# One partial sum kept in its PSUM bank, the third chunk turned first, and one count raised, in a two-layer graph network on one core

## The chip, the cores and the metric

One core of a Trainium2 chip runs the whole program; the other cores are idle. The metric is the device time of one execution in microseconds, as the median of the executions. The kernel before takes 3694.73 us (four runs beside the changed kernel, 3692.88 to 3697.72). All four, and the four of the changed kernel, are in the fast state (in the other state, called slow, a run shows a lower granted clock; one later run of the kernel before is of that kind: 5324.52 us at a clock of 0.653, against 0.991 to 0.993 in the fast runs beside it). The engines are called PE (TensorE, the matrix products), DVE (VectorE), ACT (ScalarE), POOL or GpSimd, and SP, which issues most DMA transfers.

## The reference

32 graphs of 512 nodes with 512 features, one sparse adjacency matrix for all. Two layers, each with a normalisation, ReLU, and a residual:

```python
# layer 0: attention with 8 heads of 64, masked by adj
h = maximum(layernorm(x), 0)
q, k, v = h@Wq+bq, h@Wk+bk, h@Wv+bv            # (512 x 512) @ (512 x 512) each
scores = q·k / 8 + (1 - adj) * -1e9
x = x + (softmax(scores) · v) @ Wo + bo
# layer 1: attention of the GAT kind
h = maximum(layernorm(x), 0)
hw = h @ W
e = leaky_relu(hw@a1 [:,None] + hw@a2 [None,:], 0.2) * adj
x = x + elu(softmax(e) @ hw + beta * hw)
```

All arithmetic is f32. The biases are zero in the given inputs, which one experiment below makes use of.

## The kernel before

The kernel is a software pipeline over the 32 items. In the steady state one step works on four items at once, in an order given by a string:

```python
order = {...}.get(b, "0.VDU1.rgY2.RMNH3.KQ")
# digits 0-3: a "unit": values of the last head pair, scores of this one (4 blocks of 2 heads)
# V, K, Q, M (out-projection), Y (final product): seven half-size products (Strassen's kind) each
# N: transposes of the next item   D: diagonal   g: gather   r, R: load of the residual, halves 0 and 1
# U, H: GpSimd's sums of blocks for the seven products
```

So the stretch that matters reads: final product Y, unit 2 (values, scores), the residual's second half R, out-projection M, transposes N, unit 3. PE's accumulators are PSUM banks with the tags `x`, `y`, `qz` (used by the products of seven and by scores), `s`, `po`, `pd`.

The transposes (`turn`) make four chunks: 0 and 1 in one bank pair, 2 in `po`, 3 in `qz`. ACT evicts each with a ReLU:

```python
def second():
    for c, tag in ((2, "po"), (3, "qz")):
        p = psum.tile(..., tag=tag)
        turned(p, c)                                        # 4 transposes
        nc.scalar.activation(h[1][:, c - 2, :], p, AF.Relu)
def first():
    p = psum.tile([P, 2, N], F32, tag="s")
    for c in range(2):
        turned(p[:, c, :], c)
    nc.scalar.activation(h[0], p, AF.Relu)
first(); second()
```

The final product (`final`) ends each block with an ELU. `two` first adds a second product q, into an SBUF tile of the tag `y`, which has three slots:

```python
def elu(i, k, s):
    y = wtile([P, N], tag="y", bufs=3)
    for t in range(2):
        nc.scalar.activation(y[half t], s[half t], AF.Exp, scale=...)     # L811
    nc.vector.tensor_scalar(y, y, 1.0, -1.0, min, add)                     # L814
    for t in range(2):
        nc.vector.scalar_tensor_tensor(y[half t], s[half t], ..., y[half t], mult, max)   # L816
    ...   # GpSimd adds the residual (L824), SP stores it
def two(i, k, p, q):
    s = wtile([P, N], tag="y", bufs=3)
    nc.vector.tensor_tensor(s, p, q, op=add)                               # L836
    dve(0.75)
    elu(i, k, s)
```

`dve()` runs nothing. The program is recorded once, in Python, and the recorder keeps a model clock of PE and DVE. Work that may be done at leisure is put on a list (`later(key, wait, by, cost, fn)`), and `pe()` and `dve()` advance the clocks and take from that list what fits. So a number in `dve()` sets only the order of the instructions on DVE. On that list stand, among others, the normalisations of the next item (L359), the sums of the exponentials (`es`, L579), the reciprocal of the softmax denominators in two halves (L628), and the dot products of layer 1.

The other lines that are used below: the out-projection adds its products to the residual on DVE (L675); GpSimd adds a constant row to the residual as it lands (L654), adds one of the seven products to it (L691), and makes a block sum that the last out-projection product reads (L399).

## Time and profile before

| | before |
|---|---|
| device time, median of 4 | 3694.73 us |
| span of the profiled execution | 3693.4 us |
| PE busy | 3568.2 us (97%) |
| PE not busy | 125.2 us |
| mean granted clock of TensorE | 0.991 |
| unit 2, scores, of an ordinary item | 4.84 us |
| unit 3, scores, of the same kind and size | 3.63 us |
| out-projection, of an ordinary item | 12.19 us |

The last three rows are read from the timeline of PE: the start of PE's first instruction of a phase to the start of its first instruction of the next phase, as the median of the 28 ordinary items. This start-to-start figure holds all of a delay, whether or not the profile lists a wait for it. It is the ruler of this document. The main lines of the page and of the waits are in the prediction below. What it does not show is the stretch behind unit 2, so here it is, first PE (start, duration, operation), in an ordinary item of the kernel before:

```profile
1631.23 1.08 PE L620 MATMUL pd<-es,ones 128*64 128x512 f32 x4
...
1642.50 1.90 PE L53 MATMUL qz_w<-wo,uT 128*64 128x256 f32 x16
```

The first line, the denominators' matmul, is called P0 from here on. The second is the last product of the out-projection, at P0 + 11.27. It needs the bank `qz`, which DVE has to empty first, and the block sum `uT` of GpSimd. Now DVE and GpSimd in the same stretch:

```profile
1633.50 2.30 DVE L579 TENSOR_TENSOR es<-e,e 128x1024 f32<-128x1024 f32 x1
1635.90 3.44 DVE L579 TENSOR_TENSOR es<-es,e 128x1024 f32<-128x1024 f32 x2
1639.26 1.75 DVE L628 RECIPROCAL rd<-pd 128x256 f32<-128x256 f32 x1
1640.93 0.62 DVE L675 SCALAR_TENSOR_TENSOR x<-x_w,x 128x512 f32<-128x512 f32 x1
1641.47 0.67 DVE L675 SCALAR_TENSOR_TENSOR x<-qz_w,x 128x512 f32<-128x512 f32 x1
```

```profile
1632.18 2.54 POOL L654 TENSOR_TENSOR x<-x,c_row 128x512 f32<-128x512 f32 x2 [1.78 <-DMA x<-in_x_dram]
1636.55 3.91 POOL L691 TENSOR_TENSOR x<-x,q_w 128x512 f32<-128x512 f32 x2 [1.84 <-ACT q_w L456]
1640.43 1.27 POOL L399 TENSOR_TENSOR uT<-uT,oT 128x512 f32<-128x512 f32 x1
```

DVE has no idle time here. It empties `qz` at 1641.47 + 0.67 = 1642.14, that is P0 + 10.91, and PE wants it at + 11.27. The slack is 0.36 us here, 0.30 to 0.55 in the other ordinary items at full clock (0.65 in the two at half the clock). Of it some 0.2 can be used: where DVE is the one that PE waits for, as below, PE starts 0.15 us after it. GpSimd's block sum ends at 1640.43 + 1.27 = 1641.70, P0 + 10.47, a slack of 0.80. No list of waits shows either.

One more thing about that list. The records of PE's products overlap: in an unbroken row each is 1.90 us long, but they start 1.73 apart. The list counts a wait from the end of the record before it, so it leaves out the first 0.17 us of every delay, and it drops what then comes to 0.15 or less.

### The profile page before, as it was taken

To read this page: it belongs to the slowest core of one execution; us is meant where nothing else is said; L and a number is where in the kernel's file an instruction comes from. 1 tells how busy PE (TensorE), PEld (TensorE's weight loads), DVE (VectorE), ACT (ScalarE), POOL (GpSimd) and SP (SyncE) were. 2 spreads that over 40 slices of the span, in tenths; PEclk is the share of its full clock that TensorE was granted. 3 is DMA by queue.
4 is the path that set the end of the run, shared out by engine and by line. 5 is a ranking of instruction groups with operands and counts; after the bars stand their busy time and mean duration, and the time that the engine had idled before them with its cause. 6 is when DMAs were issued, how large, how long until landed. Compare 5 with 4: busy or idle time off the path is not lost. (4 is left out here: it accounts for less than half of the span.)

```text
span 3693.4 us, 62550 instructions
## 1 busy us (share of the span) xinstructions
PE 3568.2 (97%) x25845; PEld 1977.7 (54%) x25846; DVE 2948.4 (80%) x4335; ACT 1460.8 (40%) x2310; POOL 1392.8 (38%) x1090
## 2 busy tenths in 40 slices
PE   9999999999999999999999999999999999999986
PEld 5455555555555555545555555555555555555543
DVE  7988788888887787788788887878888878878774
ACT  3333334344433444343444334444434444343432
POOL 5433244333344332443333443334433334433241
PEclk9999999999999999999999999999999999999998
DMA  3000111001111001110011110011100111100100
GB/s 129 18 26 17 38 38 35 27 17 36 38 38 35 23 19 38 38 35 27 15 38 38 38 35 22 20 38 38 35 27 18 35 38 38 35 27 15 33 26 27
DMA packets 88034, 120.81 MB, mean 33 GB/s; under 512 B 11904, under 2 KB 49792, under 8 KB 87744
## 3 DMA queue, kind: packets, MB, share of 16 engines
q1 hardware_dynamic: 86160, 114.91, 10.0%
q8 instruction: 205, 3.36, 0.4%
q10 hardware_dynamic: 1376, 1.57, 0.1%
q14 instruction: 85, 0.70, 0.1%
q0 software_dynamic: 208, 0.27, 0.0%
HBM read 83.11 MB, written 33.62 MB: 32 GB/s over the span
## 5 line engine op out<-in xcount | busy, mean ns | idle before, releaser
L634 POOL TENSOR_TENSOR oT<-oT,rd 128x512 f32<-128x512 f32 x128 | 173.1, 1352 | 1489.3 <-ACT rd L633 1489.3
L582 ACT ACTIVATE e<-e 128x1024 f32<-128x1024 f32 x512 | 534.4, 1055 | 190.9 <-DVE e L567 164.8
L555 PE MATMUL ps<-qT,kT 64*128 64x512 f32 x2048 | 497.4, 613 | 41.2 <-DVE y L816 29.6
L567 DVE SCALAR_TENSOR_TENSOR e<-maskT,ps 128x1024 f32<-128x1024 uint8 x384 | 454.4, 1211 | 84.2 <-PE ps L555 84.0
L605 PE MATMUL po<-e,v 128*64 128x512 f32 x2048 | 463.7, 594 | 22.6 <-ACT hT L415 22.6
L53 PE MATMUL pg<-at,hn 128*64 128x512 f32 x2048 | 448.8, 597 | 4.2 <-DVE dmax L788 2.1
L628 DVE RECIPROCAL rd<-pd 128x256 f32<-128x256 f32 x256 | 434.0, 1725 | 1.2 <-POOL oT L634 1.2
L579 DVE TENSOR_TENSOR es<-es,e 128x1024 f32<-128x1024 f32 x254 | 396.6, 1562 | 18.5 <-ACT e L582 1.6
L555 PEld LDWEIGHTS ps<-qT,kT 64*128 64x128 f32 x2048 | 180.4, 186 | 354.3 <-issue 219.9
L53 PEld LDWEIGHTS pg<-at,hn 128*64 128x64 f32 x2048 | 148.7, 138 | 297.8 <-issue 289.2
L605 PEld LDWEIGHTS po<-e,v 128*64 128x64 f32 x2048 | 149.1, 138 | 253.5 <-issue 214.2
L824 POOL TENSOR_TENSOR y<-y,x 128x512 f32<-128x512 f32 x124 | 157.6, 1271 | 250.9 <-DVE y L816 210.4
L654 POOL TENSOR_TENSOR x<-x,c_row 128x512 f32<-128x512 f32 x124 | 221.7, 1809 | 52.1 <-DMA x<-in_x_dram 52.1
L814 DVE TENSOR_SCALAR y<-y 128x512 f32<-128x512 f32 x128 | 61.1, 478 | 207.7 <-ACT y L811 207.7
L633 ACT ACTIVATE rd<-rd 128x512 f32<-128x512 f32 x128 | 80.7, 630 | 348.7 <-DVE rd L628 348.7
L579 DVE TENSOR_TENSOR es<-e,e 128x1024 f32<-128x1024 f32 x127 | 189.9, 1495 | 1.5 <-PE pd L620 1.5
L756 ACT ACTIVATE at<-at 128x512 f32<-128x512 f32 x128 | 80.4, 628 | 257.7 <-DVE at L752 255.1
L53 PE MATMUL qz_y<-w,vT 128*64 128x256 f32 x1520 | 180.3, 379 | 2.0 <-DVE yq L836 2.0
L729 DVE CUSTOM_DVE_ANT_0 scr<-hn,wa_r 128x512 f32<-128x512 f32 x256 | 165.6, 710 | 0.0
L562 DVE SCALAR_TENSOR_TENSOR e<-maskT,ps 128x512 f32<-128x512 uint8 x256 | 163.4, 680 | 0.0
L802 ACT COPY gT<-pg 128x512 f32<-128x512 f32 x128 | 74.3, 581 | 213.6 <-PE pg L53 213.6
L334 POOL TENSOR_TENSOR rs<-rs,mhalf 128x2 f32<-128x2 f32 (+1 forms) x97 | 78.1, 805 | 206.0 <-DVE rs L333 202.4
(221 smaller groups left out, 6470.9 us busy)
## 6 DMA issues: line engine op xcount, KB each, us to landing
x<-in_x_dram SPq DMA_DIRECT2D x128, 256.0 KB, 3.3
out_dram<-y SPq DMA_DIRECT2D x128, 256.0 KB, 2.3
x<-in_x_dram SPq DMA_DIRECT2D x63, 512.0 KB, 3.8
s<-row_s SPq DMA_DIRECT2D x32, 256.0 KB, 4.0
adj<-in_adj_dram SPq DMA_DIRECT2D x4, 256.0 KB, 7.1
wk<-in_L_gnn_Wk_dram ACTq DMA_DIRECT2D x3, 256.0 KB, 9.0
wq<-in_L_gnn_Wq_dram SPq DMA_DIRECT2D x3, 256.0 KB, 7.0
wv<-in_L_gnn_Wv_dram SPq DMA_DIRECT2D x3, 256.0 KB, 5.9
```

What stands on the lines that cost most here:

```text
L53: nc.tensor.matmul(out[s : s + HD], lhsT[:, s : s + HD], rhs, start=start, stop=stop, skip_group_check=onto)
L555: nc.tensor.matmul(ps[s], st["kT"][j][rows, ts(k, P)], st["qT"][j][rows, :], start=True, stop=True)
L562: nc.vector.scalar_tensor_tensor(e[:, s, :], maskT[:, k, :], NEG, ps[s], op0=ALU.mult, op1=ALU.add)
L567: nc.vector.scalar_tensor_tensor(e, maskT[:, k, :].unsqueeze(1).to_broadcast([P, 2, N]), NEG, p, op0=ALU.mult, op1=ALU.add)
L579: (nc.gpsimd if early else nc.vector).tensor_tensor(es, one, e, op=ALU.add)
L582: nc.scalar.activation(e, e, AF.Exp)
L605: nc.tensor.matmul(po[s * HD : (s + 1) * HD, :], v[k // 2][:, k % 2, (2 * j + s) * HD : (2 * j + s + 1) * HD], e[k][:, s, :], start=k == 0 ...
L628: nc.vector.reciprocal(rd[:, ts(k, H)], pd[:, ts(k, H)])
L634: nc.gpsimd.tensor_tensor(o, o, rd, op=ALU.mult)
L654: eng.tensor_tensor(r[:, t, :], r[:, t, :], c_row, op=ALU.add)
L729: nc.vector.tensor_tensor_reduce(scr, st["hn"][t], r, 1.0, 0.0, op0=ALU.mult, op1=ALU.add, accum_out=st["s12"][:, g, t : t + 1],)
L824: (nc.vector if b == B - 2 else nc.gpsimd).tensor_tensor(yu, yu, x_[:, :, ts(i, H)], op=ALU.add)
```

## The change

The intent: take away the two largest waits of PE. The transposes are reordered so that the bank `po` is emptied early. The sum for block (0,1) is written back into its PSUM bank, so that one tile fewer competes for the three `y` slots. And the diagonal is counted as 3.0 us instead of 2.0, which moves DVE's leisure work to later places.

```diff
-        def second():
-            for c, tag in ((2, "po"), (3, "qz")):
-                p = psum.tile([P, 1 if c == 2 else 2, N], F32, name=f"pn{c}_{b}", tag=tag)[:, 0, :]
-                turned(p, c)
-                nc.scalar.activation(h[1][:, c - 2, :], p, AF.Relu)
+        def second(c, tag):
+            p = psum.tile([P, 1 if c == 2 else 2, N], F32, name=f"pn{c}_{b}", tag=tag)[:, 0, :]
+            turned(p, c)
+            nc.scalar.activation(h[1][:, c - 2, :], p, AF.Relu)
 ... (first() unchanged)
+        if b:
+            second(2, "po")
         first()
-        second()
+        if not b:
+            second(2, "po")
+        second(3, "qz")
 ... (in diagonal)
-        dve(2.0)
+        dve(3.0)
 ... (in final)
         def two(i, k, p, q):
-            s = wtile([P, N], f"yq_{b}_{i}_{k}", "y", 3)
+
+            s = p if i == 0 else wtile([P, N], f"yq_{b}_{i}_{k}", "y", 3)
```

In the changed kernel nearly all later line numbers are higher by 3: L555 becomes L558, L567 L570, L579 L582, L628 L631, L654 L657, L675 L678, L691 L694, L811 L814, L816 L819. L836 becomes L840 and L415 L414.

## The prediction

A dip of the clock, below, is a stretch in which PE's granted clock (PEclk) is 0.50 instead of 1.00; the trace before has two in mid-run, each of 3.4 us, after waits of PE of 1.96 and 2.04 us.

> **What bounds the kernel now.** First the page of the profiled execution, for the busy shares:
>
> ```profile
> PE 3568.2 (97%) x25845; PEld 1977.7 (54%) x25846; DVE 2948.4 (80%) x4335; ACT 1460.8 (40%) x2310; POOL 1392.8 (38%) x1090
> ```
>
> PE is busy 97% of 3693.4 us, and the change adds and removes no matmul (PE's order differs only in which transposed chunk goes first). What can be won is PE's idle time, 3693.4 - 3568.2 = 125.2 us, 3.4%. So the second view is who PE waited for (total us, times, longest):
>
> ```profile
> PE ps L555 <- DVE y L816: 29.6, 29, 2.0
> PE po L605 <- ACT hT L415: 22.6, 31, 0.8
> PE pe L53 <- DVE as L763: 19.1, 2, 11.7
> PE ps L555 <- DVE e L567: 11.6, 31, 1.1
> PE y_k L53 <- ACT y_k L450: 6.3, 30, 0.3
> ```
>
> The first two are the change's targets; together 52.2 us. The third is in the tail. Next, the timeline of PE in one ordinary batch item (start, duration, operation, in brackets the wait), a cycle that repeats every 112.45 us:
>
> ```profile
> 1626.40 1.99 PE L555 MATMUL ps<-qT,kT 64*128 64x512 f32 x8
> 1629.14 2.16 PE L555 MATMUL ps<-qT,kT 64*128 64x512 f32 x8 [0.75 <-DVE y L816]
> ...
> 1644.33 1.97 PE L409 MATMUL pn<-ident,x 128*128 128x128 f32 x16
> 1647.02 3.65 PE L605 MATMUL po<-e,v 128*64 128x512 f32 x16 [0.73 <-ACT hT L415]
> ```
>
> Scores of unit 2 stop at their third block, which wants the bank pair qz; values of unit 2 stop at the bank po. Last, ACT and DVE in front of the first wait, in an item where it is 2.04 us instead of 0.75:
>
> ```profile
> 1509.88 0.91 ACT L811 ACTIVATE y<-yq,rd 128x256 f32<-128x256 f32 x2 [3.54 <-DMA out_dram<-y]
> 1512.39 0.84 ACT L811 ACTIVATE y<-qz_y,rd 128x256 f32<-128x256 f32 x2 [1.60 <-DVE y L816]
> ```
>
> ```profile
> 1507.82 0.69 DVE L836 TENSOR_TENSOR yq<-y_y,q_y 128x512 f32<-128x512 f32 x1
> 1510.88 0.43 DVE L814 TENSOR_SCALAR y<-y 128x512 f32<-128x512 f32 x1 [2.37 <-ACT y L811]
> 1511.34 0.88 DVE L816 SCALAR_TENSOR_TENSOR y<-yq,rd,y 128x256 f32<-128x256 f32 x2
> 1513.27 0.64 DVE L814 TENSOR_SCALAR y<-y 128x512 f32<-128x512 f32 x1 [1.04 <-ACT y L811]
> 1514.01 0.88 DVE L816 SCALAR_TENSOR_TENSOR y<-qz_y,rd,y 128x256 f32<-128x256 f32 x2
> ```
>
> The reader is to see that neither wait is for arithmetic. Six tiles share the three SBUF slots of the tag y. The exp of block (0,1) sits in the slot of block (0,0) and waits for that block's store; the exp of (1,0) sits in the slot of the copy yq(0,1) and waits until L816 has read it. So two blocks' ACT and DVE work runs one after the other instead of overlapped, and qz is freed at 1514.9.
>
> [...] This trace has it after the 2 us waits[...] (duration, PE busy, ..., PEclk):
>
> ```profile
> 1516.40:1519.80 3.40, 3.40 (x10) 0.77 (x8) 3.07 (x4) 3.11 (x4) 1.57 (x2) 0.50 0.93 316
> ```
>
> A second such dip is at 386.6, after a wait of 1.96. [...] the trace has 0.69 for L836 from PSUM, so I take no new cost for the add. [...] a tiny L333 took 0.77 us (1536.96 to 1537.73) and ended with POOL's L379 (1536.43 to 1537.70), against 0.17 elsewhere.
>
> **The change part by part.**
>
> (a) Transposes, 31 items (the first keeps its order). Before, ACT evicts chunks 0 and 1 together (L421, 1.02 us) and only then po (L415, half of 1.08), so po is free at 1534.5 while transposes end at 1533.84. After, chunk 2 is done a quarter in, near 1532.4, and its 0.6 us eviction ends near 1533.1, under the other transposes. The wait goes: 31 x 0.73 = 22.6 us. The whole of hT is ready when it was (about 1535.0), so GpSimd's combinations do not move.
>
> (b) q of block (0,1) in its bank. Five tiles in the three slots: exp(0,1) takes the slot of yq(1,1), long read; exp(1,0) takes that of y(0,0) and its store. In the ordinary item: the add ends 1623.90, exp(0,1) is at 1623.99 as before, exp(1,0) follows at once, 1624.8 to 1625.65 (PE's product was done at 1622.9; the store, issued at 1621.58, has landed: exp(0,1) waited for it before and was not held). DVE: L814 1624.9 to 1625.35, L816 twice to 1626.2, which frees y; L814 to 1626.65, L816 twice to 1627.6, which frees qz. PE wants y at 1627.3 and qz at 1628.2: slack 1.1 and 0.6. In the slow item the store lands near 1509.85, exp(1,0) ends 1510.7, qz is free near 1512.4 and wanted at 1512.9. So all 29.6 us go; the eleven long DMA waits no longer matter. With the two waits near 2 us go the two dips: the cycle behind each is 113.3 instead of 111.7 us (112.45 less 0.75), 1.6 us each, 3.2 us.
>
> (c) Diagonal counted 3.0 instead of 2.0. It runs nothing itself; it shifts the recorder's DVE clock. By the order of both kernels, in 28 items two of the four normalisations (L359) move from before the final product to behind the score evictions of unit 2; both halves of the reciprocal L628 now stand together before the last statistics; both L711 and the second activations of hn come behind the evictions of unit 3; the last two dot products come behind the kT evictions. In times from the pd matmul of unit 1 (before 1517.80): the last out-projection sum L675 is held by PE at +14.2 as before; statistics, two reciprocals (3.36 instead of 1.73) and statistics end near +20.85, and L333 is caught behind POOL's L380 to about +21.3. PE's first score of unit 3 is ready at 1539.33 - 1517.80 - 0.73 = +20.8. The eviction so starts 0.5 late, ends at +22.5, and the fourth score, which reuses that bank and would start at +22.35, waits 0.2. Downstream ACT has four exps and one hn before the y_k copy, ending near +28.3; PE wants it at +28.0: 0.35 instead of 0.20. Sum 0.35 us per item, 28 x 0.35 = about 10 us lost.
>
> (d) Tail. In the last but one final product exp(0,1) waited 3.04 us for the store; qz (wait 5.30) comes 2.1 earlier. In the very last, exp(0,1) waited 3.85; now exp(1,0) waits for the same landing (3683.1) and the last L816 ends near 3685.4 instead of 3688.1: 2.7. Against it, one more pair L749/L752 (0.75 + 0.69) comes behind item 30's product, before the sum PE waits 11.69 for: 1.4. Net 3.4.
>
> Sum: 22.6 + 29.6 + 3.2 + 3.4 - 10 = 48.8. 3694.9 - 48.8 = 3646.
>
> **The rivals.**
> 1. The wait moves to bank y. In-place, L816 reads y in PSUM until 1626.2 rather than the add until 1623.9, and the second score block uses y 0.9 us before the third uses qz. For it: the bank is held 2.3 us longer. Against: 1.1 us of slack above. If it took the whole 0.75, (b) would give about half: 3661.
> 2. The later dot products hold the row round trip. Its DMA is issued at +37 instead of +30.6; with 1.4 to 2.5 to write and 4.0 to read it is back at +42.5 to +43.5, and DVE reaches L749 at +42.7. For it: slack of 6 us is gone. Against: L484 to L494 have 0.8 us idle each, so up to 1 us is absorbed. Where it is not, 0.5 us in 28 items makes 3660.
> 3. The DVE loss in (c) does not occur, because L333 is not caught and each eviction keeps pace: 3636.
>
> **Range and chances.** The target waits are read off, so the doubt lies in (c) and rival 2, -10 to +15 us, and in a third clock dip more or less. 3646 us, 3634 to 3662. Faster by over 2% needs 74 us of 125, more than both targets with the tail: 0.01. Slower by over 2%: 0.01. Within 2%: 0.98.
>
> **What would show it.** Right: the two top rows gone from PE's waits; exp(0,1) on ACT no longer behind a DMA; no half-clock slice in mid-run; PE busy about 98%; the row from L567 to the scores grown from 11.6 to about 17 us and y_k from 6.3 to about 10. Wrong: scores waiting for L816 on bank y by 0.5 us or more (rival 1), L749 behind the row DMA in most items (rival 2), a new row on PE's q projections, or values of unit 2 now waiting for something else than hT.

## The result, and the profile after

The changed kernel takes 3655.45 us (four runs, 3653.69 to 3656.23), all fast. The ratio to before is 0.9892, with a 95% interval of 0.9875 to 0.9909. Ratios here are the mean time of one kernel's fast runs over that of the other's of the same rounds, so they are not quite the ratio of the medians quoted. The class is "same" at the 2% mark; the gain is about 39 us, where 49 were predicted, and the time lies inside the predicted range.

The page's busy shares, and the top of PE's waits, of the changed kernel:

```profile
PE 3565.7 (98%) x25846; PEld 1980.2 (54%) x25846; DVE 2929.3 (80%) x4335; ACT 1465.8 (40%) x2310; POOL 1422.6 (39%) x1090
```

```profile
PE pe L53 <- DVE as L766: 20.4, 2, 13.0
PE qz_w L53 <- DVE x L678: 14.5, 24, 0.8
PE ps L558 <- DVE e L570: 12.8, 33, 1.3
PE y_k L53 <- ACT y_k L453: 7.2, 30, 0.5
...
PE qz_w L53 <- POOL uT L399: 2.3, 3, 0.8
...
PE ps L558 <- DVE y L819: 0.4, 1, 0.4
```

Both targets are gone: no row for values behind hT, and of the 29 waits of the scores for L819 one of 0.4 is left. But the second row is new. In 24 items the last product of the out-projection waits for DVE's sums L678. PE in one such item:

```profile
1496.42 3.70 PE L558 MATMUL ps<-qT,kT 64*128 64x512 f32 x16
1500.06 1.08 PE L623 MATMUL pd<-es,ones 128*64 128x512 f32 x4
...
1512.13 1.95 PE L53 MATMUL qz_w<-wo,uT 128*64 128x256 f32 x16 [0.63 <-DVE x L678]
1514.01 1.97 PE L409 MATMUL pn<-ident,x 128*128 128x128 f32 x16
...
1519.49 3.97 PE L558 MATMUL ps<-qT,kT 64*128 64x512 f32 x16
```

Unit 2's scores (first line) run through without a break. The new wait sits at P0 + 12.07. The scores of unit 3 (last line) take 3.97 instead of 3.70, with no wait listed. DVE in the same stretch:

```profile
1502.19 3.03 DVE L359 TENSOR_SCALAR x<-x,mv,rs 128x512 f32<-128x512 f32 x2
1505.14 1.21 DVE L582 TENSOR_TENSOR es<-e,e 128x1024 f32<-128x1024 f32 x1
1506.46 4.32 DVE L582 TENSOR_TENSOR es<-es,e 128x1024 f32<-128x1024 f32 x2
1510.71 0.68 DVE L678 SCALAR_TENSOR_TENSOR x<-x_w,x 128x512 f32<-128x512 f32 x1
1511.31 0.67 DVE L678 SCALAR_TENSOR_TENSOR x<-qz_w,x 128x512 f32<-128x512 f32 x1
```

Against the five lines of before: the reciprocal (1.75) has left this place, a pair of normalisations L359 has come, and the pair takes 3.03 here. The first sum takes 1.21 instead of 2.30, the other two 4.32 instead of 3.44. `qz` is empty at 1511.98, P0 + 11.92 instead of + 10.91. GpSimd meanwhile:

```profile
1502.23 2.71 POOL L657 TENSOR_TENSOR x<-x,c_row 128x512 f32<-128x512 f32 x2 [3.49 <-DMA x<-in_x_dram]
1505.37 4.33 POOL L694 TENSOR_TENSOR x<-x,q_w 128x512 f32<-128x512 f32 x2 [0.44 <-ACT q_w L459]
1509.66 2.25 POOL L399 TENSOR_TENSOR uT<-uT,oT 128x512 f32<-128x512 f32 x1
```

Its row add starts 0.04 us after DVE's pair and runs beside it; its next add runs beside the sums `es`. GpSimd is held up as well: the block sum takes 2.25 instead of 1.27 and ends at 1511.91, P0 + 11.85, only 0.07 before DVE has emptied `qz`. The list names DVE because it came last; in three items it was the block sum (the row POOL uT). So PE, which in e1 below starts 0.05 after that sum, could not have started much before + 11.9 even with `qz` empty in time, and about 0.65 of the 0.8 us would have been lost all the same, an estimate from 11.85 + 0.05 against + 11.27.

ACT's two exponentials of the final product, which in the item of the prediction were 2.5 us apart, the first of them waiting for a DMA, now follow each other:

```profile
1493.82 0.84 ACT L814 ACTIVATE y<-y_y,rd 128x256 f32<-128x256 f32 x2 [2.07 <-issue]
1494.74 0.84 ACT L814 ACTIVATE y<-qz_y,rd 128x256 f32<-128x256 f32 x2
```

In the views of stretches (duration; PE, PEld, DVE, ACT, POOL busy; clock; DMA), the two places that had half the clock before have it in full, at 386.6 to 390.0 and at 1516.4 to 1519.8 (so has each of the 170 stretches of 20 us from 140 to 3540, all 1.00; before, the two with the dips have 0.91):

```profile
386.60:390.00 3.40, 3.40 (x34) 2.27 (x32) 3.29 (x5) 2.28 (x4) 1.63 (x3) 1.00 0.19 74
1516.40:1519.80 3.40, 3.40 (x18) 1.15 (x16) 3.37 (x4) 0.69 (x2) 2.75 (x3) 1.00 0.85 236
```

With the start-to-start ruler, the sums over the 28 ordinary items, in us (the median of one item in brackets):

| phase | before | after | gain |
|---|---|---|---|
| scores of unit 2 | 144.1 (4.84) | 102.6 (3.63) | +41.5 |
| denominators behind them | 26.9 | 25.4 | +1.5 |
| out-projection | 341.4 (12.19) | 363.4 (13.06) | -22.0 |
| transposes | 75.4 (2.69) | 53.1 (1.90) | +22.3 |
| scores of unit 3 | 101.8 (3.63) | 109.0 (3.90) | -7.2 |
| K projection | 349.5 (12.48) | 350.3 (12.51) | -0.8 |
| all phases of the 28 items | 3159.2 | 3123.8 | +35.4 |

The spans differ by 3693.4 - 3653.0 = 40.4, so 5.0 us come from outside the 28 items. From the start of the last ordinary GAT product (3512.11 before, 3475.03 after) to the end it is 181.3 before and 178.0 after, 3.3 of those 5.0.

The targets brought more than predicted, and the out-projection gave back 22 us that the prediction did not have.

### The profile page after: what moved, and what is told of

The parts are those of the page before. It is cut to its first block, busy times and chain, and to the rows that moved or that the text cites. A ratio compares the mean times of both kernels' runs of the same rounds, so it can differ in the third digit from the quotient of the medians.

```text
span 3653.0 us, 62549 instructions
## 1 busy us (share of the span) xinstructions
PE 3565.7 (98%) x25846; PEld 1980.2 (54%) x25846; DVE 2929.3 (80%) x4335; ACT 1465.8 (40%) x2310; POOL 1422.6 (39%) x1090
## 5 line engine op out<-in xcount | busy, mean ns | idle before, releaser
L558 PE MATMUL ps<-qT,kT 64*128 64x512 f32 x2048 | 491.5, 609 | 13.4 <-DVE e L570 12.8
L570 DVE SCALAR_TENSOR_TENSOR e<-maskT,ps 128x1024 f32<-128x1024 uint8 x384 | 453.9, 1209 | 47.4 <-PE ps L558 47.1
L582 DVE TENSOR_TENSOR es<-es,e 128x1024 f32<-128x1024 f32 x254 | 418.5, 1647 | 17.7 <-ACT e L585 1.1
L631 DVE RECIPROCAL rd<-pd 128x256 f32<-128x256 f32 x256 | 430.3, 1719 | 1.2 <-POOL oT L637 1.2
L558 PEld LDWEIGHTS ps<-qT,kT 64*128 64x128 f32 x2048 | 181.4, 186 | 320.9 <-issue 199.1
L657 POOL TENSOR_TENSOR x<-x,c_row 128x512 f32<-128x512 f32 x124 | 227.1, 1851 | 103.0 <-DMA x<-in_x_dram 103.0
L359 DVE TENSOR_SCALAR x<-x,mv,rs 128x512 f32<-128x512 f32 x128 | 102.8, 845 | 119.5 <-POOL rs L334 119.4
L582 DVE TENSOR_TENSOR es<-e,e 128x1024 f32<-128x1024 f32 x127 | 181.0, 1425 | 0.7 <-PE pd L623 0.7
```

Of the source, the lines that this page charges most:

```text
L558: nc.tensor.matmul(ps[s], st["kT"][j][rows, ts(k, P)], st["qT"][j][rows, :], start=True, stop=True)
L570: nc.vector.scalar_tensor_tensor(e, maskT[:, k, :].unsqueeze(1).to_broadcast([P, 2, N]), NEG, p, op0=ALU.mult, op1=ALU.add)
L582: (nc.gpsimd if early else nc.vector).tensor_tensor(es, one, e, op=ALU.add)
L631: nc.vector.reciprocal(rd[:, ts(k, H)], pd[:, ts(k, H)])
L657: eng.tensor_tensor(r[:, t, :], r[:, t, :], c_row, op=ALU.add)
```

## The experiments

All kernels gave correct results, and all runs of the changed kernels were fast. In the first call (e1 to e4, five rounds) the kernel before took 3695.59 (3691.81 to 3701.22, 17 runs); in the second (e5 to e8, three rounds) 3695.97 over its 18 fast runs (3693.36 to 3698.88). The 19th was slow (5324.52, clock 0.653), and no verdict uses it. The parts of the change: (a) transposes, (b) the sum in its bank, (c) the count.

The theory was that (c) makes the new wait. The rival was that (c) is neutral, as its line looks, and that (b) brought the new wait by itself, because PE comes earlier.

**e1_ab: (a) and (b) without (c).** Edit against the changed kernel:

```diff
-        dve(3.0)
+        dve(2.0)
```

> Parts (a) and (b) alone, the diagonal counted 2.0 as before. Theory (the order that the longer count makes costs about 30 us: 22 in the out-projection, 7 in the scores of unit 3, 1 in the k projection): 3622 to 3630 us, PE no longer waits for L678, scores of unit 3 back at 3.63 us per item, out-projection at 12.19. Rival (PE, freed from its two waits, simply reaches a DVE that has no time left, and the count is neutral): 3650 to 3658 us with the same wait for L678.

Measured: 3630.31 (3628.65 to 3631.50, five runs), ratio 0.9823 (0.9809 to 0.9836). It beats both kernels: 65 us under before, 25 under the changed kernel (that one from another call). The time is 0.3 us above the range of my theory. PE's waits:

```profile
PE pe L53 <- DVE as L766: 19.0, 2, 11.6
PE ps L558 <- DVE e L570: 12.2, 32, 1.3
PE y_k L53 <- ACT y_k L453: 6.3, 30, 0.4
```

No row for L678. The scores of unit 3 are back to 3.63. So in company with (a) and (b), the count costs 25 us. One thing is left: the out-projection takes 12.41, not the 12.19 that I expected. In one item, GpSimd and PE:

```profile
1501.65 1.27 POOL L399 TENSOR_TENSOR uT<-uT,oT 128x512 f32<-128x512 f32 x1
```

```profile
1491.53 1.08 PE L623 MATMUL pd<-es,ones 128*64 128x512 f32 x4
...
1502.97 1.95 PE L53 MATMUL qz_w<-wo,uT 128*64 128x256 f32 x16
```

The last product starts at P0 + 11.44, 0.05 after GpSimd has ended the block sum it reads. That is 0.17 late, just what the list leaves out, so no wait is listed for it.

**e2_c: (c) alone, on the kernel before.**

```diff
-        dve(2.0)
+        dve(3.0)
```

> Only the longer count, on the kernel before. Theory: slower by 25 to 30 us (3720 to 3725), with the out-projection lengthened by 0.8 us and the scores of unit 3 by 0.25 per item though both old waits are still there. Rival (the loss needs the earlier PE): 3693 to 3698, no wait for L678.

Measured: 3694.79 (3691.66 to 3697.82, 13 runs), ratio 0.9997 (0.9988 to 1.0005). My expectation of a loss was wrong. Alone, the count costs nothing that these runs can resolve: the interval reaches from a gain of 4 us to a loss of 2. The order of DVE is the one of the changed kernel, though. DVE in one item, whose P0 is at 1517.37, and GpSimd:

```profile
1519.63 2.09 DVE L359 TENSOR_SCALAR x<-x,mv,rs 128x512 f32<-128x512 f32 x2
1521.64 1.21 DVE L579 TENSOR_TENSOR es<-e,e 128x1024 f32<-128x1024 f32 x1
1522.96 4.32 DVE L579 TENSOR_TENSOR es<-es,e 128x1024 f32<-128x1024 f32 x2
1527.20 0.68 DVE L675 SCALAR_TENSOR_TENSOR x<-x_w,x 128x512 f32<-128x512 f32 x1
1527.80 0.67 DVE L675 SCALAR_TENSOR_TENSOR x<-qz_w,x 128x512 f32<-128x512 f32 x1
```

```profile
1518.46 2.51 POOL L654 TENSOR_TENSOR x<-x,c_row 128x512 f32<-128x512 f32 x2 [1.93 <-DMA x<-in_x_dram]
```

GpSimd's row add starts at P0 + 1.09 here (median 0.91) and is half done when the pair comes, so the pair takes 2.09 instead of 3.03. `qz` is empty at 1528.47, P0 + 11.10, still before + 11.27. With (b), PE is some 1.2 us earlier, the residual's load is not (it is issued behind the final product's stores), and the row add starts at P0 + 2.22 in the median. The refined theory: the loss needs (b) and (c) together. It is GpSimd's two adds falling upon the pair and the sums that use up the slack. e5 to e7 test this. That it is (b), and not (a), which (c) needs beside it is argued from the timeline alone: neither pair was run.

**e3_a: (a) alone.** (The transposes' part of the diff, with `dve(2.0)` and the SBUF tile for the sum.)

```diff
-            s = p if i == 0 else wtile([P, N], f"yq_{b}_{i}_{k}", "y", 3)
+            s = wtile([P, N], f"yq_{b}_{i}_{k}", "y", 3)
-        dve(3.0)
+        dve(2.0)
```

> Only the order of the transposes. Both theories: faster by 22 to 24 us (3671 to 3673), the wait of the values for hT gone, the wait of the scores for L816 still 29 to 30 us in total, the two half-clock slices in mid-run perhaps elsewhere. If much less is gained, the wait had only moved.

Measured: 3676.29 (3668.59 to 3680.30, five runs), ratio 0.9946 (0.9932 to 0.9959): a gain of 19 to 20 us, where I expected 22 to 24. The runs spread over 12 us, four times as far as those of e1, and the cause of the shortfall stays open. The profiled execution spans 3670.1, 23.3 less than before's; its transposes take 53.1 us in the 28 items, as in the changed kernel, and the other wait stands:

```profile
PE ps L558 <- DVE y L819: 30.1, 29, 2.3
```

**e4_b: (b) alone.** (Before, with the one line of `two` changed.)

```diff
-            s = wtile([P, N], f"yq_{b}_{i}_{k}", "y", 3)
+            s = p if i == 0 else wtile([P, N], f"yq_{b}_{i}_{k}", "y", 3)
```

> Only q of block (0,1) in its bank. Theory: the scores of unit 2 go from 4.84 to 3.63 us in an ordinary item, more in the eleven slow ones: 43 us in the 28 items with the half-clock slices, 3 to 5 more at the end: 3645 to 3650. If the gain is only the 30 us that the waits list, 3662 to 3665.

Measured: 3654.48 (3650.99 to 3655.72, four runs), ratio 0.9888 (0.9873 to 0.9903), a gain of 41 us. It is a little outside what I expected. The scores of unit 2 gain 42.4 us in the 28 items, and the out-projection loses 6.1 (12.41 each), the same GpSimd delay as in e1. So one line of the change brings as much as the whole change.

**e5_abc_less_pool: the changed kernel with less work on GpSimd.** In the ordinary items the row add L657 is left out for the residual's second half. The row is zero for these inputs, so the result stays right; as a kernel for other biases it would be wrong.

```diff
-            for t in range(n):
+            for t in range(n if i == 0 or not 2 < b < B - 2 else 0):
                 eng.tensor_tensor(r[:, t, :], r[:, t, :], c_row, op=ALU.add)
```

> The changed kernel with one cost taken away: GpSimd's addition of the constant row to the second half of the residual (about 2.7 us per item, in items 3 to 29; the row is zero for these inputs, so the result stays right). The order on the other engines is that of the changed kernel. Theory now (DVE is late at the out-projection's sums because its normalisations and sums of exponentials are blocked by GpSimd's additions, which come later against PE than before): the pair of L359 shrinks from 3.0 to about 1.5 us, the out-projection from 13.06 to 12.2 or 12.4 per item: 3632 to 3642 us. Rival (DVE simply has the two instructions more, GpSimd doesn't matter): W stays near 13.0, 3652 to 3656.

Measured: 3633.61 (3632.56 to 3634.06, four runs), ratio 0.9832 (0.9815 to 0.9848). DVE's order is that of the changed kernel:

```profile
1493.99 1.00 DVE L359 TENSOR_SCALAR x<-x,mv,rs 128x512 f32<-128x512 f32 x2
1494.90 1.22 DVE L582 TENSOR_TENSOR es<-e,e 128x1024 f32<-128x1024 f32 x1
1496.22 3.44 DVE L582 TENSOR_TENSOR es<-es,e 128x1024 f32<-128x1024 f32 x2
1499.94 0.69 DVE L678 SCALAR_TENSOR_TENSOR x<-x_w,x 128x512 f32<-128x512 f32 x1 [0.28 <-PE x_w L53]
```

The pair takes 1.00 instead of 3.03, the last two sums 3.44 instead of 4.32, and DVE comes to the first sum before PE has its product. The out-projection is back at 12.19, and 21 of the 22 us are back. The scores of unit 3 keep 3.90: that loss has another cause. GpSimd gains too: in this item its block sum ends at P0 + 10.17 instead of + 11.85. So e5 shows that the clash with the row add is the cause, but not which of the two held-up engines would have held PE alone.

**e6_ab_pair_late: e1 with only the pair in the late place.** In the code of the normalisations, on top of `dve(2.0)`:

```diff
-                    later(("x", b), more, more + 5.0, 0.55, lambda u=u: second(u))
+                    late = b > 3 and u > 1
+                    later(("x", b), more + (14.0 if late else 0.0), more + 5.0, 0.0 if late else 0.55, lambda u=u: second(u))
```

> On (a) and (b): only the pair L359 behind the evictions of unit 2, everything else on DVE as with the count of 2.0, so the first half of the reciprocal still stands in front of the out-projection's sums. Theory: DVE comes 1.7 us later still to those sums than in the changed kernel: out-projection about 14.5 to 15 instead of 13.06, scores of unit 3 about 3.63: 3680 to 3700 us. Rival (only the pair's own 1 us counts): 3645 to 3655.

Measured: 3693.20 (3686.39 to 3700.45, 16 runs), ratio 0.9994 (0.9986 to 1.0001): all that (a) and (b) gain is lost. PE's largest wait, and DVE in one item:

```profile
PE qz_w L53 <- DVE x L679: 53.9, 28, 2.3
```

```profile
1517.04 1.97 DVE L360 TENSOR_SCALAR x<-x,mv,rs 128x512 f32<-128x512 f32 x2
...
1525.57 1.74 DVE L632 RECIPROCAL rd<-pd 128x256 f32<-128x256 f32 x1
1527.24 0.62 DVE L679 SCALAR_TENSOR_TENSOR x<-x_w,x 128x512 f32<-128x512 f32 x1
```

Now pair and half reciprocal both stand in front of the sum. The out-projection takes 14.66.

**e7_ab_recip_late: e1 with only the reciprocal in the late place.** The pair stays in front of the final product; both halves of the reciprocal come behind the out-projection's sums, as in the changed kernel.

```diff
-            later("rd", 0.0, gap(b, (j + 1) % NP) + 3.0, 1.7, lambda k=k: divide(k))
+            later("rd", 13.0 if (j == 1 and 1 < b < B - 1) else 0.0, gap(b, (j + 1) % NP) + 3.0, 1.7, lambda k=k: divide(k))
```

> On (a) and (b): both halves of the reciprocal behind the last sums, as in the changed kernel, but the pair L359 stays in front of the final product. Theory: out-projection 12.2 to 12.4, scores of unit 3 lengthened by 0.26 as in the changed kernel: 3632 to 3640 us. Rival (reciprocals are the cause of the out-projection's loss): 3650 or more.

Measured: 3637.72 (3636.30 to 3639.38, four runs), ratio 0.9844 (0.9828 to 0.9861). The out-projection takes 12.41 as in e1, the scores of unit 3 take 3.91 as in the changed kernel. So the two moves of (c) are told apart, all on top of (a) and (b) (medians of different calls, beside each of which the kernel before took 3694.7 to 3696.0):

| | pair early | pair late |
|---|---|---|
| half reciprocal before the sums | 3630 (e1) | 3693 (e6) |
| both halves behind them | 3638 (e7) | 3655 (the changed kernel) |

The late pair costs 63 us where the reciprocal stays, 18 where it has made room. The late reciprocal, with the small instructions that move along with it, costs 7 by itself, which is the scores of unit 3.

**e8_ab_u_later: a try at a better kernel.** In e1, GpSimd's block sums U one unit later, to relieve that engine:

```diff
-        }.get(b, "0.VDU1.rgY2.RMNH3.KQ")
+        }.get(b, "0.VD1U.rgY2.RMNH3.KQ")
```

> A try at something better: (a) and (b), and GpSimd's combinations of the attention output taken behind the scores of unit 1, so that half a reciprocal no longer stands between the diagonal and the evictions of unit 1. The scores of unit 1 take 4.25 us per item against 3.63 elsewhere; if that goes and GpSimd is in time for the gathered products: 3612 to 3618 us. If GpSimd is late then, a new wait in Y: 3630 or more.

Measured: 3774.79 (3771.00 to 3777.73, four runs), ratio 1.0215 (1.0198 to 1.0232), clock 0.981. It is slower, clear of noise, though the interval straddles the 2% mark, and far from both numbers that I expected. PE:

```profile
PE pd L623 <- DVE rd L631: 116.2, 30, 3.9
```

U asks for the reciprocal before it starts; moved, it lets the recorder put the second half of the reciprocal behind unit 1's evictions, and the next denominators' matmul waits for the bank `pd` in 30 items. The try failed for a reason that has nothing to do with GpSimd.

What was not tried: loading the residual's second half earlier, so that GpSimd's row add is over before the pair comes. It needs a fourth residual buffer; whether SBUF has room for it was not shown by a build. So e5 takes the row add away, and no version with the row add at another time was run.

## Why the prediction was right or wrong

The time lies in the range and the class is right. The sum has two errors of opposite sign: the targets were put 10 us too low, the losses 20 us too low. That the first makes up for half of the second is luck.

**(a) right.** Predicted 22.6 for all 31 items. The transposes gained 22.3 in the 28 ordinary items, 0.80 each for 0.73; e3 has the same figure for (a) alone.

**(b) right in mechanism, too small in size.** Predicted 29.6 for the waits and 3.2 for the clock dips, 32.8 together. Measured: 43.0 in the 28 items (41.5 in the scores, 1.5 in the denominators). The prediction took the sum of listed waits as the size of the stall. The timeline of PE that it quotes has the difference: from 1626.40 to 1629.14, 2.74 us for the first two of four scores, where an undisturbed half is 3.63 / 2 = 1.82; and from there to P0, 2.09 for the second two. That is 0.92 and 0.28 too long, 1.20 together, for one listed wait of 0.75. The list leaves out 0.17 of the 0.92, and the whole of the 0.28; that the fourth score there waits for the late eviction of the second is argued from the shared bank, not shown. Both dips went, as predicted.

**(c) the term that failed.** The two losses that the prediction named are there, about as big as it said: unit 3's scores 0.27 each (predicted 0.2), the K projection 0.03 (predicted 0.15), 8.0 us together for 10. In the list of waits they hardly show: the row of L570 grew to 12.8, where about 17 was expected, and that of y_k to 7.2 instead of 10. It missed the third, 22.0 us in the out-projection. The step is the sentence "the last out-projection sum L675 is held by PE at +14.2 as before". It is true to the letter: in the changed kernel that sum is held by PE, at 1514.11 - 1500.06 = + 14.05. But PE itself is held, by the second sum. The + 14.2 came from the item at 1517.80, the one with half the clock behind its 2 us wait. In an item at full clock the same sum runs at 1644.45 - 1631.23 = + 13.22. In the item with half the clock PE wants the bank `qz` at 1530.04 - 1517.80 = + 12.24, and a bank that DVE frees at + 11.92 looks early enough; at full clock PE wants it at + 11.27. So the ruler was 0.97 us too long, just at the place where the slack is 0.36.

With that ruler, two of the prediction's own facts were not put to use: that two normalisations move in front of the sums, and that a DVE instruction can take longer beside one of GpSimd (its L333 took 0.77 us and ended with GpSimd's L379, against 0.17 elsewhere). e5 shows the weight of the second: without the row add the pair takes 1.00 instead of 3.03, and 21 of the 22 us are back. e6 and e7 show the first: with the pair early, there is no such loss. And e2 shows that the count alone is harmless, because PE then comes late enough and GpSimd's row add is half over. Of the 22.0, some 6 come with (b) even without (c), through GpSimd's late block sum (e1, e4), and 16 with (c). In those 16 DVE and GpSimd are late together, each slower where the other runs too (the pair 3.03 for 1.00, the block sum 2.25 for 1.27), and the prediction looked at neither's slack here.

**(d) right in the net, partly by luck.** From the last ordinary GAT product to the end the gain is 3.3, predicted 3.4. Its negative part shows too: the wait for L766 grew from 19.1 to 20.4, by 1.3 for the predicted 1.4. But without (c), in e1, that stretch takes 175.1: a gain of 6.2 where 4.8 (2.1 + 2.7) was predicted. So (c) cost 2.9 there, twice the 1.4, and the two errors cancel.

**The rivals.** Rival 1 (the wait moves to bank y) is refuted: one wait of 0.4. Rival 2 (the row's round trip holds L752, the old L749) did not happen: DVE came to L752 128 times and waited for the row once (4.8 us, in the tail; before, 5.0), and no wait of PE's q projections is in the list. Rival 3 (no loss) is refuted by e1, which is 25 us faster. What did happen was in none of them.

**The sum.** 43.0 + 22.3 - 7.2 - 0.8 - 22.0 = 35.3 in the 28 items, and 5.0 outside: 40.3, against 40.4 between the profiled spans.

## What to carry to other kernels

Before a change moves work in front of an instruction, measure the slack of that instruction in an undisturbed item: here slacks of 0.36 us at DVE and 0.80 at GpSimd, listed nowhere, decided 22 us, and an item with half the clock hid the first. Look at all that the instruction needs: a list of waits names the engine that came last, and another may have come only 0.07 us before it. Measure a stall from the start of one phase to the start of the next, not from the listed waits. And try the parts of a change one at a time and in pairs: the version without the count is 25 us faster than the whole, while the count alone is neutral.

## What the traces show of the hardware

- Stretches of 3.4 us with the clock at 0.50 followed waits of PE of 1.96 and 2.04 us, and went when those waits went; a wait of 2.02 elsewhere in the kernel before was not followed by one (1.00 in the 3.4 us from its end). In e6, of 21 waits of 2.04 to 2.29 us, two were followed by a slower PE: the product behind them took 3.43 and 2.53 us instead of 1.95. What decides between them stays open.
- Two normalisations of 128x512 on DVE took 1.00 us without GpSimd's row add (e5), 2.09 beside the second half of it (e2) and 3.03 beside all of it (the changed kernel). Two f32 sums of 128x1024 took 2.55 with no add of GpSimd beside them but for the last 0.4 us (before, at 1521.93), 3.44 where GpSimd's next add began during the first of them and 4.32 where it was running already.
- The reciprocal of 128x256 in f32 takes 1.7 us, more than the two normalisations of 128x512 in e5 (1.00).
- A list of PE's waits leaves something out. Where the records of products overlap by 0.17 us, one wait of 0.75 stood for 1.20, the scores of unit 3 grew by 0.27 each without any listed wait, and GpSimd's late block sum cost 0.17 in e1 without one.
